# Moving the first norm's squares, small steps and table copies between engines, and deeper fetching in the second convolution

## The chip, the cores and the metric

The kernel runs on one core of a Trainium2 chip. A core has a matrix engine (TensorE, PE in the profile), a vector engine (VectorE, DVE), an activation engine (ScalarE, ACT), a general engine (GpSimd, POOL) and an engine that here only issues transfers (SyncE, SP). They work in parallel, each through its own instructions in order, and wait for each other through semaphores. The metric is the device time of one execution in microseconds. The kernel before took 2557.08 us, the median of three runs (2556.99 to 2560.38).

## The reference

The input x holds 128 images of 128 channels by 16 x 16 points. The part that matters here is the first layer:

- an adaptive group norm of each image: the mean and variance of four channels together, `xn = (x - m) / sqrt(v + eps)`,
- a batch norm over all images, clip to 0..1, rounding to 4 bits, a 3 x 3 convolution with 4-bit weights masked by a pattern,
- a second batch norm, clip, rounding and 3 x 3 convolution with another pattern,
- the sum of that with the normed input as the result of the layer.

The batch norm's mean and variance over all images follow from each image's statistics, so the first convolution can't start before all of x has been read. The layer after it (a two-way state-space mixer with four heads, and a mixture of eight experts) takes the rest of the time.

## The kernel before

**Layout.** Channels lie on the 128 partitions. x stays in the chip's memory as 64 tiles `xr[i]` of two images each (256 KB).

**Setup and first norm (L344 to L511).** SP issues the small inputs, the weights w1 (L364), 64 loads of x (L371), all later weights (`load_weights`, L278 to L307, called at L399), w2 (L401), and then the stores of two tables, `rows_d` and `cols_d` (L489, L490). The tables `rows0` and `cols0` are written by GpSimd (`patterns`, L376 to L397) out of `heads`, `triple`, `ident` and `far`; they go to HBM because the last stage needs copies of them in memory that is not free yet.

For each image VectorE computes statistics (`bn_stats`, L443). For every fourth image below 120 ScalarE does that in two passes: a sum (L441) and, with the negated mean from VectorE (`neg`, L453), a square with a sum (L457). The images are taken in four groups, cut at 48, 96 and 120. ScalarE first takes all sums of a group, then all its squares. For each group VectorE then has some fifteen small steps on tiles of 128 x (images of the group) (L462 to L480), with two matmuls by `grp` (L472, L478) that average over four channels; ScalarE takes the square root (L481), and `normed` (L420 to L434) refines its inverse and derives the scale and shift. `normed` of one group is placed behind the statistics of the next. The last passes (L495 to L511) join all images into the scale `sc1` and shift `bi1` of the first quantising step.

Between these steps VectorE, ScalarE and GpSimd also prepare w1 (`conv_weights`, L138 to L185: tanh, scaling, rounding, masking, and a split into three bf16 parts). The last step writes `how1`, which says which of three forms of the convolution is needed. `by_weights` (L223) reads it on every engine and branches.

**First convolution (conv1, L514).** Per tile: ScalarE or GpSimd applies scale and shift into `q` (L525, L527), VectorE clips and rounds into a padded tile `hpad` (L192), TensorE does five matmuls (L218), ScalarE moves the result to memory (L541), VectorE takes statistics (L542), and SP stores it (L544), except the first eight tiles, which are kept. w2 is prepared along the way. conv1's pools take memory that the setup's pool gives back, the tables among it.

**Second convolution (conv2, L605).** Per tile: SP fetches the stored tile (`fetch`, L618, five tiles ahead, six buffers), ScalarE scales and shifts it in place (L622), VectorE quantises (L192), TensorE convolves (L218), GpSimd or ScalarE prepares the normed input (L663, L665), VectorE adds (L666), TensorE transposes the result (L631), ScalarE copies it into one of three buffers `yt` (L633), and SP stores it (L635). Some steps of the second weights and of the next layer's first tiles are placed between.

**The long stage** (from about 294 us to the end) follows an order written out by hand (the table `T`, L1200). The order in the stages before it is the scheduler's: each engine's list follows the program's order and estimated times, and `tc.issue_after(x)` places steps no earlier than behind x.

Of the kernel before, what the change touches and what calls it, by code (L numbers as in the profile page):

```python
# [34 lines left out]
def kernel(ctx: ExitStack, tc: tile.TileContext, a: dict):  # L35
# [60 lines left out]
    nc.gpsimd.memset(heads, 0.0)  # L96
    nc.gpsimd.memset(triple, 0.0)
    for m in range(2):
        for q in range(3):
            for t in (3 + 4 * q, 15 + 4 * q):  # L100
                nc.gpsimd.affine_select(
                    out=heads, in_=heads, pattern=[[-1, NH]], compare_op=ALU.not_equal,
                    fill=-1.0, base=-(64 + 32 * m + t), channel_multiplier=1,
                )
            nc.gpsimd.affine_select(
                out=triple[:, m : m + 1], in_=triple[:, m : m + 1], pattern=[[0, 1]], compare_op=ALU.not_equal,
                fill=1.0, base=-(64 + 32 * m + q), channel_multiplier=1,
            )
# [114 lines left out]
    def by_weights(how, phase, taps):  # L223

        some = nc.values_load(how[0:1, 0:1], min_val=0, max_val=2)
        with tc.If(some > 0) as cmp:
            with tc.If(some > 1) as cmp2:
                phase(range(9), 3)
            with cmp2.Else():
                phase(range(9), 1)  # L230
        with cmp.Else():
            phase(taps, 1)
# [111 lines left out]
    with tc.tile_pool(name="w1p", bufs=1) as w1p:  # L344

        grp = w1p.tile([P, P], F32, name="grp")
        nc.gpsimd.affine_select(
            out=grp, in_=ones, pattern=[[-4, 32], [0, 4]], compare_op=ALU.is_ge, fill=0.0,
            base=0, channel_multiplier=1,
        )  # L350
        nc.gpsimd.affine_select(
            out=grp, in_=grp, pattern=[[4, 32], [0, 4]], compare_op=ALU.is_ge, fill=0.0,
            base=3, channel_multiplier=-1,
        )
        nc.vector.tensor_scalar(grp, grp, 0.25, None, ALU.mult)
# [4 lines left out]
        with tc.tile_pool(name="setup1", bufs=1) as setup, tc.tile_pool(  # L360
            name="psa", bufs=1, space=PSUM
        ) as psa:
            w1 = w1p.tile([P, 9, P], F32, name="w1", tag="w")
            nc.sync.dma_start(w1, a["L0_conv_w1"])  # L364
            weights = conv_weights(wq1, how1, w1p, psa, w1, pat1, CROSS, "c1")
            for _ in range(3):
                next(weights)


            for i in range(NP):  # L370
                nc.sync.dma_start(xr[i], x_c[:, 2 * i : 2 * i + 2, :])  # L371
            rows0 = setup.tile([P, NH, 2, 2, P], BF16, name="rows0")
            cols0 = setup.tile([P, 2, 2, 2, 2, P], BF16, name="cols0")
            far = setup.tile([HD, 1], BF16, name="far")

            def patterns():  # L376
                nc.gpsimd.memset(far, -1e30)
                for h in range(NH):
                    nc.gpsimd.tensor_copy(
                        rows0[:, h].rearrange("p d t l -> p (d t l)"), heads[:, h : h + 1].to_broadcast([P, 4 * P])  # L380
                    )
                    nc.gpsimd.tensor_copy(
                        rows0[0:HD, h].rearrange("p d t (f l) -> p (d t f) l", l=HD),
                        ident[0:HD, 0:HD].unsqueeze(1).to_broadcast([HD, 2 * 2 * 2, HD]),
                    )
                for m in range(2):
                    for d in range(2):
                        sign = 1 - 2 * d
                        nc.gpsimd.tensor_copy(
                            cols0[:, m, d].rearrange("p j f l -> p (j f l)"), triple[:, m : m + 1].to_broadcast([P, 4 * P])  # L390
                        )
                        for half in range(2):
                            nc.gpsimd.affine_select(
                                out=cols0[0:HD, m, d, :, half, :], in_=far.unsqueeze(2).to_broadcast([HD, 2, P]),
                                pattern=[[0, 2], [sign, P]], compare_op=ALU.is_ge, fill=0.0,
                                base=-sign * HD * half - 1, channel_multiplier=-sign,
                            )  # L397

            load_weights()  # L399
            w2 = w1p.tile([P, 9, P], F32, name="w2", tag="w")  # L400
            nc.sync.dma_start(w2, a["L0_conv_w2"])  # L401

# [11 lines left out]
            cuts = [0, 3 * B // 8, 3 * B // 4, B - max(B // 16, 1), B]  # L414

            def by_scalar(b):

                return b % 4 == 3 and b < cuts[3]

            def normed(c):  # L420

                of = slice(cuts[c], cuts[c + 1])
                var_, gm_, dev_, ga_, qv_, dm_ = (t[:, of] for t in (var, gm, dev, ga, qv, dm))
                nc.vector.reciprocal(ga_, ga_)
                nc.vector.tensor_tensor(dm_, ga_, ga_, ALU.mult)
                nc.vector.tensor_tensor(dm_, dm_, qv_, ALU.mult)
                nc.vector.tensor_scalar(dm_, dm_, -0.5, 1.5, ALU.mult, ALU.add)
                nc.vector.tensor_tensor(ga_, ga_, dm_, ALU.mult)
                nc.vector.scalar_tensor_tensor(shift[:, of], gm_, -1.0, ga_, ALU.mult, ALU.mult)
                nc.gpsimd.tensor_scalar(ares[:, of], ga_, 1.0, SCALE, ALU.add, ALU.mult)  # L430
                nc.gpsimd.tensor_scalar(bres[:, of], shift[:, of], SCALE, None, ALU.mult)
                nc.vector.tensor_tensor(dev_, dev_, ga_, ALU.mult)
                nc.vector.tensor_tensor(var_, var_, ga_, ALU.mult)
                nc.vector.tensor_tensor(var_, var_, ga_, ALU.mult)  # L434

            for c in range(4):
                of = slice(cuts[c], cuts[c + 1])
                for b in range(B)[of]:
                    x_b = xr[b // 2][:, b % 2, :]
                    if by_scalar(b):  # L440
                        nc.scalar.activation(junk, x_b, AF.Copy, accum_out=bst[:, b, 1:2])  # L441
                    else:
                        behind = nc.vector.bn_stats(bst[:, b, :], x_b)  # L443
                if c > 0:

                    with tc.issue_after(behind.ins):
# [3 lines left out]
                if mine:  # L450

                    picked = slice(mine[0], cuts[c + 1], 4)
                    nc.vector.tensor_scalar(neg[:, picked], bst[:, picked, 1], -1.0 / NT, None, ALU.mult)  # L453
                    nc.vector.tensor_scalar(bst[:, picked, 1], neg[:, picked], -1.0, None, ALU.mult)
                    nc.vector.tensor_scalar(bst[:, picked, 4], neg[:, picked], -1.0, None, ALU.mult)
                    for b in mine:
                        nc.scalar.activation(  # L457
                            junk, xr[b // 2][:, b % 2, :], AF.Square, bias=neg[:, b : b + 1],
                            accum_out=bst[:, b, 2:3],
                        )  # L460

                nc.vector.tensor_tensor(mean_, bst[:, of, 1], bst[:, of, 4], ALU.add)  # L462
                nc.vector.tensor_scalar(mean_, mean_, 0.5, None, ALU.mult)
                nc.vector.tensor_tensor(dm_, bst[:, of, 1], bst[:, of, 4], ALU.subtract)
                nc.vector.tensor_tensor(dm_, dm_, dm_, ALU.mult)
# [846 lines left out]
```

## Time and profile before

| | us |
|---|---|
| median of three runs | 2557.08 |
| the profiled execution | 2554.94 |
| its span, first to last instruction | 2553.1 |
| first convolution's first step (ScalarE q) | 85.72 |
| end of the first convolution's statistics (VectorE mv) | 171.4 |
| second convolution's first matmul | 174.74 |
| last transposing of the second convolution | 292.35 |

| engine | busy us | share of the span |
|---|---|---|
| TensorE | 2415.3 | 95% |
| VectorE | 2253.2 | 88% |
| ScalarE | 2173.0 | 85% |
| GpSimd | 1629.3 | 64% |

The shares are averages over stages with different limits. In the first 60 us TensorE is hardly used, the transfers are, and VectorE and ScalarE follow them. The times above are the starts of instructions in the trace, counted from the span's start. A busy time can hold a wait inside an instruction; the idle time before an instruction, and what ended it, are shown apart.

### The profile page before, as it was taken

The page shows a single profiled execution, that of the slowest core. Times are in us where ns is not written, and L with a number is a line of the kernel's source. Part 1 is how long each engine was busy: PE and PEld are TensorE (multiplying, and loading weights), DVE is VectorE, ACT ScalarE, POOL GpSimd, SP SyncE. Part 2 cuts the span into 40 slices and gives each one's busy share as a digit, 9 for nine tenths or more (in the row PEclk, how much of TensorE's full clock was granted, in tenths as well). Part 3 has the DMA queues.
Part 4 walks back from the last instruction along what each step waited for, and adds up shares of the span by engine and source line. Part 5 has one row for each costly group of instructions (what it writes and reads, how often), then busy time and mean ns, then how long its engine had stood idle before and what let it go on. Part 6 is the DMA issues. An engine that isn't in the chain of part 4 may idle for free.

```text
span 2553.1 us, 49290 instructions
## 1 busy us (share of the span) xinstructions
PE 2415.3 (95%) x15940; PEld 1479.9 (58%) x15940; DVE 2253.2 (88%) x6163; ACT 2173.0 (85%) x4455; POOL 1629.3 (64%) x1694
## 2 busy tenths in 40 slices
PE   0688889999999999999999999999999999999997
PEld 0235456666666666666666666666666666666663
DVE  8787699999999999999999999999999999999883
ACT  5678699888889998889898888998988899898881
POOL 3468026676666666666666666666667666666666
PEclk9999899999999999999999999999999999999998
DMA  9358633434444444444444344444433443443343
GB/s 287 124 192 281 227 67 110 125 111 123 130 124 122 122 125 118 120 132 128 120 126 124 114 119 129 128 121 119 129 118 117 132 132 121 123 123 116 107 125 107
DMA packets 302167, 339.58 MB, mean 133 GB/s; under 512 B 56768, under 2 KB 226752, under 8 KB 301888
## 3 DMA queue, kind: packets, MB, share of 16 engines
q1 hardware_dynamic: 301888, 336.21, 43.3%
q8 instruction: 133, 2.18, 0.3%
q14 instruction: 146, 1.20, 0.2%
HBM read 262.72 MB, written 56.62 MB: 125 GB/s over the span
## 4 chain that ended last, share of the span: by engine, by line
PE 88%; DMA 4%; DVE 3%; ACT 2%; issue 1%; SPq 1%; POOL 1%; POOLq 0%; ACTq 0%; DVEq 0%
PE f_ps L1189 17%; PE x_ps L877 13%; PE y_ps L1012 10%; PE z_ps L920 9%; PE o_ps L1072 9%; PE sg L965 5%; PE xt_ps L932 4%; PE y_ps L1018 4%; PE g_ps L951 4%; PE cv L218 4%; DMA xr<-in_x 2%; PE n_ps L1045 1%; PE u_ps L1094 1%; PE f_ps L1184 1%; PE u_ps L750 1%
## 5 line engine op out<-in xcount | busy, mean ns | idle before, releaser
L1177 POOL TENSOR_TENSOR gb<-gb,u2T 128x512 f32<-128x512 f32 x512 | 641.3, 1277 | 122.7 <-PE y_ps L1018 68.8
L895 DVE SCALAR_TENSOR_TENSOR xc<-x_ps,cw,xc 128x510 f32<-128x510 f32 (+2 forms) x768 | 571.7, 744 | 46.5 <-ACT xc L889 36.9
L1028 POOL TENSOR_TENSOR yg<-yg,z 128x512 f32<-128x512 f32 x256 | 325.9, 1279 | 352.1 <-DVE yg L1024 155.1
L1189 PE MATMUL f_ps<-gb,ew 128*128 128x512 f32 x1024 | 510.1, 602 | 6.7 <-POOL gb L1177 6.4
L877 PE MATMUL x_ps<-uT,wx 128*128 128x512 f32 x768 | 402.9, 607 | 7.6 <-ACT e L731 3.3
L731 ACT ACTIVATE e<-sg 128x512 f32<-128x512 f32 x512 | 299.3, 591 | 49.9 <-PE sg L965 44.4
L731 ACT ACTIVATE e<-e,ends 128x128 f32<-128x128 f32 x1024 | 325.0, 392 | 0.0
L1012 PE MATMUL y_ps<-e,xt 128*64 128x256 f32 x2048 | 317.8, 389 | 0.2 <-DVE yg L1024 0.2
L993 DVE TENSOR_TENSOR e<-e,g_ps 128x1024 f32<-128x1024 f32 x256 | 311.6, 1217 | 5.5 <-ACT e L731 2.4
L895 DVE SCALAR_TENSOR_TENSOR bc<-x_ps,cw,bc 128x510 f32<-128x510 f32 (+2 forms) x384 | 286.7, 747 | 20.5 <-ACT bc L889 4.1
L1189 PEld LDWEIGHTS f_ps<-gb,ew 128*128 128x128 f32 x1024 | 180.5, 192 | 174.2 <-issue 136.2
L920 PE MATMUL z_ps<-uT,wz 128*128 128x512 f32 x512 | 271.2, 611 | 1.5 <-ACT xc L889 1.0
L889 ACT ACTIVATE xc<-x_ps,cb,cw 128x512 f32<-128x512 f32 x256 | 199.0, 777 | 64.0 <-PE x_ps L877 57.4
L1072 PE MATMUL o_ps<-wo,yg 128*128 128x128 f32 x2048 | 251.4, 276 | 0.2 <-DVE e L998 0.2
L1072 PEld LDWEIGHTS o_ps<-wo,yg 128*128 128x128 f32 x2048 | 240.5, 193 | 11.1 <-DVE g L1149 8.4
L1024 DVE SCALAR_TENSOR_TENSOR yg<-xc,dcol,y_ps 128x512 f32<-128x512 f32 x256 | 189.8, 742 | 50.1 <-PE y_ps L1018 46.8
L1060 POOL TENSOR_TENSOR rr<-rr,mhalf 128x8 f32<-128x8 f32 x64 | 109.9, 1718 | 161.7 <-DVE g L1151 82.7
L1018 PE MATMUL y_ps<-e,xt 128*64 128x128 f32 x2048 | 199.0, 273 | 0.0
L965 PE MATMUL sg<-rows,cols 128*128 128x256 bf16 x1024 | 192.1, 274 | 5.8 <-ACT e L731 2.8
L1018 PEld LDWEIGHTS y_ps<-e,xt 128*64 128x64 f32 x2048 | 147.0, 137 | 74.1 <-DVE e L998 0.5
L218 PE MATMUL cv<-hpad,wq 128*128 128x512 bf16 x640 | 161.7, 396 | 19.5 <-DVE hpad L192 19.4
L1012 PEld LDWEIGHTS y_ps<-e,xt 128*64 128x64 f32 x2048 | 118.9, 136 | 100.9 <-issue 53.8
(256 smaller groups left out, 4813.9 us busy)
## 6 DMA issues: line engine op xcount, KB each, us to landing
gb<-gd SPq DMA_DIRECT2D x256, 512.0 KB
e<-cum SPq DMA_DIRECT2D x256, 256.0 KB
xr<-in_x SPq DMA_DIRECT2D x64, 256.0 KB
cc<-bc SPq DMA_DIRECT2D x128, 128.0 KB
out<-ob SPq DMA_DIRECT2D x64, 256.0 KB
y<-yt SPq DMA_DIRECT2D x60, 256.0 KB
yt<-y SPq DMA_DIRECT2D x60, 256.0 KB
o<-o SPq DMA_DIRECT2D x56, 256.0 KB
```

The lines of the kernel that those rows point to most:

```text
L731: nc.scalar.activation(out, in_, func, **more)
L877: nc.tensor.matmul(ps, wx[d][:, n * P : (n + 1) * P], uTs[i], start=True, stop=True)
L895: nc.vector.scalar_tensor_tensor(acc[:, :, to], raw[:, :, of], cw[:, d, n, 3 - back : 4 - back], acc[:, :, to], ALU.mult, ALU.add,)
L920: nc.tensor.matmul(ps, wz[:, d, n * P : (n + 1) * P], uTs[i], start=True, stop=True)
L965: nc.tensor.matmul(sg[:, :, of], c_[:, k, d, s, half, :], r_[:, :, d, s, of], start=True, stop=True)
L993: nc.vector.tensor_tensor(e0.rearrange("p h t l -> p h (t l)"), e0.rearrange("p h t l -> p h (t l)"), gps[i, d, k][:, 0:NT].unsqueeze(1).t ...
L1012: nc.tensor.matmul(y_ps[64 * q : 64 * q + 64, k, :], xt[:, 2 * k + s0, 64 * h : 64 * h + 64], e0[:, h].rearrange("p t l -> p (t l)"), star ...
L1018: nc.tensor.matmul(y_ps[64 * q : 64 * q + 64, k, s1 * P : (s1 + 1) * P], xt[:, 2 * k + s1, 64 * h : 64 * h + 64], e1[:, h, :], start=False ...
L1028: large(nc.gpsimd.tensor_tensor(yg, yg, zs[i, d][:, n, :], ALU.mult))
L1072: nc.tensor.matmul(o_ps[:, (2 * j + d) * P : (2 * j + d + 1) * P], ygs[i, d, n][:, t * P : (t + 1) * P], wo[d][:, n, :], start=(n == 0), s ...
L1177: large(nc.gpsimd.tensor_tensor(gb[:, e], gb[:, e], u2Ts[i], ALU.mult))
L1189: nc.tensor.matmul(f_ps, ew[:, e, :], gbs[i, e], start=False, stop=(e == NE - 1))
```

## The change

- Squares: ScalarE takes the square of an image right after the sum of the next one of its images, no longer all squares behind all sums of a group. Each image has its own negation `neg`, on GpSimd.
- Groups: three in place of four, cut at 48 and 112; ScalarE has 28 images in place of 30.
- Small steps: for the first two groups the steps between statistics and scale are GpSimd's, with fused steps taken apart; for the last group they stay on VectorE. ScalarE copies `gm` out of the matmul's result and adds eps itself.
- The reciprocals of the first two groups are placed behind a certain image's statistics, image 78 for the first and image 126 for the second.
- The last six passes (`rs` to `bi1`) are GpSimd's; two products (`b15`, `g15`) are made early.
- Tables: `heads` and `triple` are sums over parts of `ident` on VectorE; `far` is a wider tile; ScalarE copies all of `rows0` and `cols0`, before and after the tanh of w1. Their stores and w2's load are issued right behind x, ahead of `load_weights`.
- `grp` is scaled on GpSimd.
- The kind of weights, `kind(how1)`, is read into registers in the program where `how1` is known.
- conv2: fetches eight tiles ahead, ten buffers.

```diff
-    nc.gpsimd.memset(heads, 0.0)
-    nc.gpsimd.memset(triple, 0.0)
-    for m in range(2):
...
+    strips = ident[:, HD:].rearrange("p (m r) -> p m r", r=32)
+    nc.vector.tensor_reduce(heads, strips[:, :, 3:27].rearrange("p m (u h) -> p h m u", h=NH), AX.XY, ALU.add)
+    nc.vector.tensor_scalar(heads, heads, -1.0, None, ALU.mult)
+    nc.vector.tensor_reduce(triple, strips[:, :, 0:3], AX.X, ALU.add)
...
-        nc.vector.tensor_scalar(grp, grp, 0.25, None, ALU.mult)
+            nc.gpsimd.tensor_scalar(grp, grp, 0.25, None, ALU.mult)
+            far = setup.tile([HD, 2, HD + P], F32, name="far")
...
+            def patterns():
+                nc.scalar.copy(
+                    rows0[:HD].rearrange("p h d j (f l) -> p (h d j f) l", l=HD),
+                    ident[:HD, :HD].unsqueeze(1).to_broadcast([HD, 8 * NH, HD]),
+                )
+                nc.scalar.copy(
+                    rows0[HD:].rearrange("p h d j l -> p h (d j l)"), heads[HD:].unsqueeze(2).to_broadcast([HD, NH, 4 * P])
+                )
+                last = nc.scalar.copy(
+                    cols0[HD:].rearrange("p m d j f l -> p m (d j f l)"), triple[HD:].unsqueeze(2).to_broadcast([HD, 2, 8 * P])
+                )
+                yield last
+                for d in range(2):
+                    for half in range(2):
+                        for m in range(2):
+                            nc.scalar.copy(
+                                cols0[:HD, m, d, :, half, :],
+                                far[:, d, HD - HD * half : HD - HD * half + P].unsqueeze(1).to_broadcast([HD, 2, P]),
+                            )
+                yield
...
             for i in range(NP):
                 nc.sync.dma_start(xr[i], x_c[:, 2 * i : 2 * i + 2, :])
-            load_weights()
+            nc.sync.dma_start(rows_d, rows0)
+            nc.sync.dma_start(cols_d, cols0)
             w2 = w1p.tile([P, 9, P], F32, name="w2", tag="w")
             nc.sync.dma_start(w2, a["L0_conv_w2"])
+            load_weights()
...
-            cuts = [0, 3 * B // 8, 3 * B // 4, B - max(B // 16, 1), B]
+            cuts = [0, 3 * B // 8, 7 * B // 8, B]
...
+                eng = nc.vector if c == 2 else nc.gpsimd
+                eng.tensor_tensor(dm_, ga_, ga_, ALU.mult)
+                eng.tensor_tensor(dm_, dm_, qv_, ALU.mult)
+                eng.tensor_scalar(dm_, dm_, -0.5, 1.5, ALU.mult, ALU.add)
...
+            def squares(most):
+
+                while waiting and most:
+                    b = waiting.pop(0)
+                    nc.scalar.activation(
+                        junk, xr[b // 2][:, b % 2, :], AF.Square, bias=neg[:, b : b + 1], accum_out=bst[:, b, 2:3]
+                    )
+                    most -= 1
...
                     if by_scalar(b):
                         nc.scalar.activation(junk, x_b, AF.Copy, accum_out=bst[:, b, 1:2])
+                        nc.gpsimd.tensor_scalar(neg[:, b : b + 1], bst[:, b, 1:2], -1.0 / NT, None, ALU.mult)
+                        squares(1)
+                        waiting.append(b)
                     else:
-                        behind = nc.vector.bn_stats(bst[:, b, :], x_b)
...
+                        last = nc.vector.bn_stats(bst[:, b, :], x_b)
+                    if b in (cuts[1] + 30, B - 2):
+                        with tc.issue_after(last.ins):
+                            nc.vector.reciprocal(ga[:, cuts[c - 1] : cuts[c]], ga[:, cuts[c - 1] : cuts[c]])
                         normed(c - 1)
...
+                    squares(len(mine))
+                    nc.gpsimd.tensor_scalar(bst[:, picked, 1], neg[:, picked], -1.0, None, ALU.mult)
+                    nc.gpsimd.tensor_scalar(bst[:, picked, 4], neg[:, picked], -1.0, None, ALU.mult)
...
-                nc.vector.tensor_copy(gm_, gm_ps)
-                nc.vector.tensor_tensor(dev_, mean_, gm_, ALU.subtract)
+                nc.scalar.copy(gm_, gm_ps)
+                eng.tensor_tensor(dev_, mean_, gm_ps if c == 2 else gm_, ALU.subtract)
...
-                nc.vector.tensor_scalar(qv_, gv_ps, EPS, None, ALU.add)
-                nc.scalar.activation(ga_, qv_, AF.Sqrt)
+                nc.scalar.activation(ga_, gv_ps, AF.Sqrt, bias=epsc)
+                if c == 2:
+                    nc.vector.tensor_scalar(qv_, gv_ps, EPS, None, ALU.add)
+                    nc.vector.reciprocal(ga_, ga_)
+                else:
+                    nc.scalar.activation(qv_, gv_ps, AF.Identity, bias=epsc)
...
-            rsqrt_eps(rs, bv, EPS)
-
-            nc.vector.tensor_scalar(rs, rs, gam1, NLEV, ALU.mult, ALU.mult)
...
+            nc.gpsimd.tensor_scalar(rs, bv, EPS, None, ALU.add)
+            nc.gpsimd.tensor_tensor(rs, rs, mhalf[:, 0:1], ALU.pow)
+            nc.gpsimd.tensor_tensor(rs, rs, g15, ALU.mult)
+            nc.gpsimd.tensor_scalar(sc1, ga, rs, None, ALU.mult)
+            nc.gpsimd.tensor_scalar(bi1, shift, bm, rs, ALU.subtract, ALU.mult)
+            nc.gpsimd.tensor_scalar(bi1, bi1, b15, None, ALU.add)
...
-                    qs[i] = pc.tile([P, 2, NT], F32, name=f"q2_{i}", tag="q")
+                    qs[i] = pc.tile([P, 2, NT], F32, name=f"q2_{i}", tag="q", bufs=10)
...
-            for i in range(5):
+            for i in range(8):
                 fetch(i)
...
-                fetch(i + 5)
+                fetch(i + 8)
```

## The prediction

> **What bounds the kernel now.** I first read the page: TensorE is busy 95% of the span, and the chain of waits is 88% TensorE. From about 340 us on, a hand-ordered TensorE-bound stage runs to the end. The diff touches nothing there, so what it can move is the time at which that stage starts. Two stages come before it: the load of x with the first norm and first convolution (0 to 172 us), and the second convolution (172 to 292 us). I read the timeline of the first (start, duration, engine, line, tile; in brackets the idle time before and what ended it).
>
> ```profile
> 11.14 7.84 DVE L355 TENSOR_SCALAR grp<-grp 128x128 f32<-128x128 f32 x1
> ...
> 37.95 2.09 DVE L474 TENSOR_TENSOR dev<-mean,gm 128x48 f32<-128x48 f32 x1
> ...
> 61.44 0.24 DVE L466 TENSOR_TENSOR var<-bst 128x48 f32<-128x48 f32 x1 [0.28 <-ACT junk L457]
> ...
> 68.95 0.17 DVE L462 TENSOR_TENSOR mean<-bst 128x8 f32<-128x8 f32 x1
> ...
> 77.33 0.29 DVE L511 TENSOR_SCALAR bi<-bi,b 128x128 f32<-128x128 f32 x1
> ...
> 79.74 0.43 SPq L489 DMA_DIRECT2D rows_d<-rows  x1
> ...
> 85.72 3.23 ACT L525 ACTIVATE q<-xr,bi,sc 128x256 f32<-128x256 f32 x6 [13.64 <-DMA rows_d<-rows]
> ```
>
> The norm is finished at 77.62 (L511), but the first operation of conv1 starts at 85.72: its buffers reuse the setup memory, and the store of rows0 from there is issued at 79.74, behind all weight loads in SP's queue. So 8.1 us are a wait for a late store. Before that VectorE lost 7.8 us at L355 while GpSimd worked, and reached its last image at 68.9. The chain of waits over the load gives what the stage could reach:
>
> ```profile
> 5.02 5.12 DMA xr<-in_x
> 10.15 5.94 DMA xr<-in_x
> ...
> 46.53 6.00 DMA xr<-in_x
> 52.55 6.34 DMA ew<-in_L_ffn_expert_w
> ```
>
> Eight tiles of 256 KB land every 6.0 us, one per 0.75 us: tile k at about 9.4 + 0.75k, tile 63 at about 56.8. VectorE's last image is 12 us behind it.
>
> For the second convolution I took the waits between 178 and 290 us (total, times, longest) and its part of the chain:
>
> ```profile
> DVE xr L666 <- PE cv L218: 17.4, 32, 1.4
> ACT q L622 <- DMA q<-o: 13.7, 16, 1.5
> PEld yt_ps L631 <- ACT yt L633: 9.6, 13, 1.2
> ```
> ```profile
> 194.44 4.92 DMA q<-o
> 199.44 0.67 ACT q L622
> ...
> 214.91 4.55 DMA q<-o
> ...
> 227.89 4.21 DMA q<-o
> ```
>
> ScalarE waits 13.7 us for fetched tiles; TensorE then waits for ScalarE's copies (yt). When nothing waits, the additions L666 come 1.545 us apart. Their first is at 178.88 and the 64th at 291.5: 112.6 us for 63 steps instead of 97.3, so 15.3 us are lost.
>
> **What the Trainium skill says.** GPSIMD Engine Reference, 1 Specifications: GpSimd shares its SBUF interfaces with VectorE, with contention for VectorE instructions in a two-port mode or with two SBUF inputs. The trace agrees: L355 lasts 7.84 us beside GpSimd's table writes, L474 2.09 us beside L184's 2.36 us, where their like take 0.2 to 0.3. ScalarE: Activation LUTs, What ACT_TABLE_LOAD costs: 186 ns + 0.833 ns per element; for 1152 elements that is 1.15 us, and L169 took 1.152. DMA: Bandwidth & Descriptors, Where 436 GB/s comes from: about 358 GB/s per core to HBM; the load of x ran at 349. Advanced Engine Details and Errata, Control Flow Timing: a compare-and-branch costs about 108 ns; but GpSimd's first work of conv2 starts 4.4 us after its last of conv1 ("issue" in the timeline, 173.4 to 177.77), and that number is used.
>
> **The first stage, part by part.** The instruction order of the built kernel says where each step sits.
>
> Tables. GpSimd loses 12 + 6 selections, 12 table copies and 8 selections (about 14 us); ScalarE gets three copies of 2048 elements (each 0.19 + 1.71 = 1.9 us, estimate from the skill's price) and eight of 256 (0.31 apart, near the 0.42 of L441's form). Table load to 2.06, copies to 7.8, tanh as before at 8.68 because w1 lands then, eight small copies to 12.4. Tile 1 landed at 10.15, so ScalarE starts 2.2 us late. VectorE starts at 9.4 instead of 18.9, for the scaling of grp is on GpSimd. It has 100 statistics of 0.335 us (33.5 us) and about 9.5 us of w1's steps in a 47 us load: it stays near the arrivals.
>
> ScalarE in the load. A sum and a square follow each other at 0.54 and 0.63 us, 1.17 per image against 1.50 per arrival, so it catches up by about 20 us. Then it meets steps queued in its order: the cast of w1 waits for VectorE's w, which comes after tile 24 (27.4) plus 1.35: 29.3, done at 30.4. A sum and two squares: 32.2. Its new copy of gm waits for five GpSimd steps (0.35 each, below) and a matmul: 33.9. Two sums, the 1.28 us table load, sqrt and the second copy: 36.8. Square and cast: 38.6; then the third cast waits for GpSimd's 2.36 us subtraction and ends at 42.2. Tile 33, next in line, landed at 34.2. Left are 12 sums and 14 squares: 6.5 + 8.8 = 15.3, to 57.5. GpSimd's eleven steps for the first group stand before some of its negations, which ScalarE's squares need: 1 us more, 58.5. So ScalarE, not the load, ends the second group.
>
> GpSimd steps. No row has 128x64 on it. Nearest rows:
>
> ```profile
> L596 POOL TENSOR_TENSOR nmra<-mva,rstda 128x4 f32<-128x4 f32 x64 | 15.3, 240 | 4.9
> L431 POOL TENSOR_SCALAR bres<-shift 128x48 f32<-128x48 f32 x2 | 0.7, 344 | 0.2
> L184 POOL TENSOR_TENSOR w<-t_c,wq 128x1152 f32<-128x1152 f32 x2 | 4.9, 2448 | 18.7 <-ACT wq L183 18.7
> ```
>
> Between 0.24 and about 0.52 (the line through 1.28 for 512 elements and 2.36 for 1152), I take 0.35 with gaps, and 0.6 as the bad end for contention. After the sum of tile 55 (57.2): negation and five steps to the mean, 59.3; matmul and ScalarE's copy, 60.2; five steps, 62.0; matmul and sqrt, 62.9. VectorE's reciprocal (0.55) stands before its last statistics, so that statistic, waiting behind the sqrt though its tile landed at 56.8, ends at 63.9. From there the last group took 68.95 to 75.61 before, 6.7 us; I add 0.7 for ScalarE's copy and for VectorE's two-input steps beside GpSimd's eleven for group two (63.5 to 67.4): 71.3. The last six passes on GpSimd: 0.2, 0.58 (the power, L133), 0.26, three of 128x128 at about 0.4, gaps 0.5: 2.7, where VectorE with the power took 2.0. So 74.0, and conv1 at 74.1: a gain of 11.6.
>
> Stores of the tables. They now stand right behind x in SP's queue, are issued when tile 56 has landed (52.6) and took 5.9 us before: down by about 60. w2 waits for w1's last cast (42.2), no delay at 53; the small weights go to 79 as now, and the first store of conv1 is wanted only at tile 8, about 85. Cost nothing; if SP were later, five o1 buffers cover 6 us.
>
> GpSimd's jump into conv1 now comes after its last pass: first work 4.3 us after the start instead of 1.3. Tile 3 is its first; the first ten matmuls took 4.28 us (87.33 on) and tile 3 was due 7 us in: cost nothing, 2 us if not covered. The early read of the kind of weights changes no engine's order: nothing. Conv1 itself is unchanged.
>
> **The second convolution.** Ten fetch buffers for six. A buffer comes free when its tile is quantised, then 4 to 5 us of fetch: six tiles at 1.545 are 9.3 us, and ScalarE runs ahead of the quantising VectorE by one or two tiles; ten give 15.5. At the start SP stood 12.7 us before it could fetch on (DMA at 0 to 94 GB/s around 181 to 189 us); four more tiles use that gap. Between zero and all 13.7 us can go. Of the 15.3 lost I count as the fetches' the stalls at 199 (1.9), 219 (2.5), 232 (about 2), 245 to 252 (about 1.7 of 4.9, the rest is the early norm's GpSimd and ScalarE steps) and 269 (0.9): 9.0. Full pace needs 512 KB per 1.545 us, 339 GB/s, near the 349 seen, so I don't take more.
>
> **Sum.** 11.6 + 9.0 = 20.6 us, carried through to the end since TensorE bounds the rest. The profiled execution took 2554.94 (span 2553.1 and 1.8 around it): 2534.3. The median of the runs is 2.1 above it: 2536.5.
>
> **Rivals.** (1) The fetches aren't cured, because stores and fetches share a saturated DMA: 0.7 to 0.89 busy speaks for it, streaks of seven tiles at 1.545 against. Only 11.6 remain: 2545.5. (2) GpSimd becomes the bound of the norm: seventeen of its small steps lie on the path to 74; at 0.7 us each instead of 0.35, 6 us more: 2542.5. The 2.09 us of L474 speaks for contention; the nmra row against. (3) Slower: a y store needs one of three yt buffers. Its turn is its landing time L plus 1 us for copy and issue; three buffers give (L+1)/3 per tile. The chain shows L = 3.63 at 247.5 (1.54). If fetches in flight stretch L, conv2 loses more than conv1's start gained from 1.84 + 11.6/64 = 2.02 us per tile, L = 5.1; at L = 6, 2.33 x 64 = 149 against 117.6: 2577. Against it: one fetch per tile is issued as before, only earlier. (4) ScalarE keeps up and the load bounds: 56.8 + 0.5 + 6.7 + 2.2 = 66.2, 8 us better, with all 13.7 of conv2: 2524. (5) The change doesn't take effect: conv1's first step still waits, for a later load counted on the same queue, about 85: only conv2's 9 remain, 2548.
>
> **How the numbers follow.** The forecast has 0.62 (14 to 27 us: 2530 to 2543), rival 1 0.12, rival 2 0.08, rival 4 0.08, rival 3 0.05, rival 5 and the mixtures with under 5 us of gain 0.05. This kernel's measurement can't tell 0.2% (5.1 us) from nothing. All but the last two are faster: 0.90, same 0.05, slower 0.05. The range 2527 to 2547 leaves out half of rival 4, rival 3, rival 5 and a part of the forecast's edges.
>
> **What would show it.** ScalarE's first q of conv1 near 74, its wait ended by GpSimd's bi and not by rows_d; VectorE's first statistics near 9.5; ScalarE's last square of the second group near 58; small GpSimd steps near 0.35; conv2's steps near 1.65 us and ACT q's wait for q under 4 us. I am wrong if y stores take over 5 us, if VectorE's steps after 62 us stretch beside GpSimd, or if the long stage starts earlier but ends no earlier.

## The result and the profile after

The changed kernel takes 2543.47 us, the median of four runs (2541.67 to 2545.61), against 2557.30 for the kernel before beside it (four runs, 2556.99 to 2560.38). The ratio is 0.9944, with a 95% interval of 0.9926 to 0.9961: 13.8 us faster. I had forecast 20.6. The time lies in the range; both parts of the sum are smaller than I had them, and one of them for a reason that I had not seen. It also lies just outside 2530 to 2543, where I had put the forecast itself: the range holds it because it was left wide for the rivals.

| | before | after | earlier by |
|---|---|---|---|
| profiled execution, its span | 2554.94, 2553.1 | 2543.71, 2542.0 | 11.1 (span) |
| conv1's first step (ScalarE q) | 85.72 | 75.79 | 9.9 |
| conv1's first matmul | 87.33 | 77.40 | 9.9 |
| VectorE starts to join conv1's statistics (mv) | 169.47 | 159.28 | 10.2 |
| first addition of conv2 | 178.88 | 167.94 | 10.9 |
| 64th addition of conv2 | 291.46 | 279.31 | 12.2 |
| end of conv2's last copy yt | 293.66 | 281.51 | 12.2 |

The first stage gave 9.9 us in these two executions, conv2 1.2 from its first to its 64th addition (112.6 to 111.4). The 171.4 that I gave for mv ahead of the prediction is its end, not its start. The profiled execution of before was 2.4 us below the median of its four runs, that of after at its own. The long stage, which no version here touches, took 2258.6 to 2262.1 us in the profiles of this study (from the end of conv2's last copy yt to the end of the span), so two single executions can't be compared to better than about 3.5 us.

The timeline of the changed kernel's first stage (start, duration, engine, line, tile; in brackets the idle time before and what ended it):

```profile
9.60 1.10 DVE L469 BATCH_NORM_STATS2 bst<-xr 128x6 f32<-128x256 f32 x3 [4.18 <-DMA xr<-in_x]
...
32.32 1.50 POOL L483 TENSOR_TENSOR mean<-bst 128x48 f32<-128x48 f32 x1
...
35.16 0.20 ACT L495 COPY gm<-gm_ps 128x48 f32<-128x48 f32 x1 [2.42 <-PE gm_ps L494]
...
58.27 0.42 ACT L464 ACTIVATE junk<-xr 128x256 f32<-128x256 f32 x1
...
59.56 0.51 ACT L453 ACTIVATE junk<-xr,neg 128x256 f32<-128x256 f32 x1
...
61.51 0.36 POOL L488 TENSOR_TENSOR var<-bst 128x64 f32<-128x64 f32 x1
...
64.61 0.55 DVE L472 RECIPROCAL ga<-ga 128x64 f32<-128x64 f32 x1 [7.17 <-ACT ga L502]
...
65.08 0.37 DVE L469 BATCH_NORM_STATS2 bst<-xr 128x6 f32<-128x256 f32 x1
...
74.23 0.81 POOL L532 TENSOR_SCALAR bi<-shift,bm,rs 128x128 f32<-128x128 f32 x1
75.14 0.61 POOL L533 TENSOR_SCALAR bi<-bi,b 128x128 f32<-128x128 f32 x1
75.79 3.06 ACT L547 ACTIVATE q<-xr,bi,sc 128x256 f32<-128x256 f32 x6 [7.09 <-POOL bi L533]
```

VectorE starts 9.3 us sooner (18.90 before). The last line is what the change did to the stage: the first q follows the norm's last pass within 0.1 us, where it had stood 8.1 us more for the store of `rows_d`. That store is now issued at 51.88. The lines of L483 and L495 and GpSimd's last two, L532 and L533, are where it came short of the forecast.

The waits in conv2 of the changed kernel, between 168 and 280 us (total, times, longest):

```profile
DVE xr L688 <- PE cv L209: 15.6, 31, 1.3
ACT yt L655 <- PE yt_ps L653: 13.6, 14, 2.5
ACT q L644 <- DMA q<-o: 8.0, 9, 2.3
PEld yt_ps L653 <- ACT yt L655: 5.8, 9, 2.1
```

and the fetches and stores in its chain of waits:

```profile
200.55 4.17 DMA q<-o
...
215.50 5.39 DMA q<-o
...
237.60 3.77 DMA y<-yt
```

ScalarE still waits 8.0 us for fetched tiles, and fetches still stand in the chain at places (205, 220) where TensorE waits for copies yt, although ten tiles can now be under way.

### The profile page after: what moved, and what is told of

Read it like the earlier page. It is cut to its first block, busy times and chain, and to the rows that moved or that the text cites. A ratio compares the mean times of both kernels' runs of the same rounds, so it can differ in the third digit from the quotient of the medians.

```text
span 2542.0 us, 49262 instructions
## 1 busy us (share of the span) xinstructions
PE 2412.9 (95%) x15936; PEld 1481.2 (58%) x15936; DVE 2239.5 (88%) x6094; ACT 2178.8 (86%) x4462; POOL 1639.8 (65%) x1733
## 4 chain that ended last, share of the span: by engine, by line
PE 90%; DVE 3%; ACT 2%; issue 1%; DMA 1%; POOL 1%; SPq 0%; ACTq 0%; POOLq 0%; DVEq 0%
PE f_ps L1211 17%; PE x_ps L899 13%; PE y_ps L1034 10%; PE z_ps L942 9%; PE o_ps L1094 9%; PE sg L987 5%; PE xt_ps L954 4%; PE y_ps L1040 4%; PE g_ps L973 4%; PE cv L209 4%; PE n_ps L1067 1%; PE u_ps L1116 1%; PE f_ps L1206 1%; PE u_ps L772 1%; PE rt_ps L1123 1%; PE yt_ps L653 1%
## 5 line engine op out<-in xcount | busy, mean ns | idle before, releaser
L917 DVE SCALAR_TENSOR_TENSOR bc<-x_ps,cw,bc 128x510 f32<-128x510 f32 (+2 forms) x384 | 286.5, 746 | 20.6 <-ACT bc L911 4.5
L1094 PEld LDWEIGHTS o_ps<-wo,yg 128*128 128x128 f32 x2048 | 240.5, 193 | 11.1 <-DVE g L1171 8.4
L1040 PEld LDWEIGHTS y_ps<-e,xt 128*64 128x64 f32 x2048 | 147.0, 137 | 74.1 <-DVE e L1020 0.5
L209 PE MATMUL cv<-hpad,wq 128*128 128x512 bf16 x640 | 162.3, 398 | 12.8 <-DVE hpad L183 12.7
```

Source lines behind the costliest of these rows:

```text
L917: nc.vector.scalar_tensor_tensor(acc[:, :, to], raw[:, :, of], cw[:, d, n, 3 - back : 4 - back], acc[:, :, to], ALU.mult, ALU.add,)
L1040: nc.tensor.matmul(y_ps[64 * q : 64 * q + 64, k, s1 * P : (s1 + 1) * P], xt[:, 2 * k + s1, 64 * h : 64 * h + 64], e1[:, h, :], start=False ...
L1094: nc.tensor.matmul(o_ps[:, (2 * j + d) * P : (2 * j + d + 1) * P], ygs[i, d, n][:, t * P : (t + 1) * P], wo[d][:, n, :], start=(n == 0), s ...
```

## The question, and what the order shows

Each tile k of conv2 has a fetch, an activation q on ScalarE and, when its convolution is added, a copy yt, also on ScalarE. The instruction order of the built kernels tells how they stand in ScalarE's list. In the steady part of the form that ran, the last q ahead of the copy yt of tile j is that of tile j + 8 (sometimes j + 9) before, and of tile j + 12 (sometimes j + 13) after. Four more buffers, and the scheduler put q four tiles further ahead. Measured from tile to tile, the time from a fetch's issue to the start of its q is 5.0 us on average before and 6.4 after, and from q to the quantising step on VectorE 5.2 before and 10.6 after. Most of the new slack lies behind q, where nobody waits for a transfer. The timeline of the changed kernel shows what it costs (lines of ScalarE, then of TensorE):

```profile
220.49 0.81 ACT L644 ACTIVATE q<-q,bi,sc 128x512 f32<-128x512 f32 x1 [2.27 <-DMA q<-o]
221.21 0.57 ACT L655 ACTIVATE yt<-yt_ps 128x512 f32<-128x512 f32 x1
...
221.84 0.66 PE L653 MATMUL yt_ps<-ident,xr 128*128 128x128 f32 x4 [1.57 <-ACT yt L655]
```

The q here is tile 40's, quantised only at 235.19. The copy behind it is tile 28's, added at 215.75, and TensorE, which needs its bank of the matmul memory, stands 1.57 us for it. ScalarE stands in order at a fetch that nothing needs for another 14 us. This is the largest stall of conv2: the addition of tile 32 follows the one before it after 7.23 us, where the steady step is 1.545.

So theory A: the order on ScalarE ate the deeper fetch. Its rivals: theory B, the deeper fetch brought its 9 us and another part of the change lost 7; theory C, my rival of the saturated DMA.

## Experiments on the second convolution

**Fetch depth undone.** The changed kernel with six buffers.

```diff
-                    qs[i] = pc.tile([P, 2, NT], F32, name=f"q2_{i}", tag="q", bufs=10)
+                    qs[i] = pc.tile([P, 2, NT], F32, name=f"q2_{i}", tag="q")
...
-            for i in range(8):
+            for i in range(5):
...
-                fetch(i + 8)
+                fetch(i + 5)
```

> The changed kernel with six fetch buffers and five tiles fetched ahead in the second convolution, as in the kernel before. Theory A (the order on ScalarE ate the deeper fetch: its rescaling of tile k stands 12 tiles ahead of the copy yt with ten buffers, 8 with six, so a fetch has about 4.5 us either way): almost nothing is lost, first to 64th addition about 112.5 us instead of 111.4, time 2544 to 2546. Theory B (ten buffers did bring the 9 us that I forecast, and another part of the change cost 7 us in conv2): the loss is the whole 9, about 2552.

Measured: 2547.80 us (2544.22 to 2549.09, six runs), ratio to before 0.9965 (0.9953 to 0.9978). That is 4.3 us above the changed kernel. It lies between the theories, nearer A; theory B's 2552 is excluded. The depth was worth some 4 us, and since the two ratios have intervals of this width, anything from nothing to 10 us is possible. In its profiled execution, the highest of the six, ScalarE waited 18.6 us for q and the additions spread over 117.9 us. That is 5.3 us more than in the profile of the kernel before, with the same six buffers and again a lead of 8 tiles. What made that one execution longer is open, so the weighing of A against B here rests on the medians; the experiments on the order decide it.

**ScalarE's order mended.** The changed kernel with ten buffers; q of tile k may not stand ahead of the copy yt of tile k-7.

```diff
+            yts_done = {}
...
                 q = qs.pop(i)
-                nc.scalar.activation(q, q, AF.Identity, bias=bi2, scale=sc2)
+                if i - 7 in yts_done:
+                    with tc.issue_after(yts_done[i - 7].ins):
+                        nc.scalar.activation(q, q, AF.Identity, bias=bi2, scale=sc2)
+                else:
+                    nc.scalar.activation(q, q, AF.Identity, bias=bi2, scale=sc2)
...
-                nc.scalar.activation(yt.rearrange("p t c -> p (t c)"), yt_ps, AF.Copy, scale=1.0 / SCALE)
+                yts_done[i] = nc.scalar.activation(yt.rearrange("p t c -> p (t c)"), yt_ps, AF.Copy, scale=1.0 / SCALE)
```

> The changed kernel, with ScalarE's rescaling of tile k of conv2 put behind its copy yt of tile k-7 in its own order; ten buffers stay. Theory A: ScalarE no longer stands at a fetch that it does not need yet (its waits for q fall from 8.0 us to under 1), the copies yt come in time, and first to 64th addition falls from 111.4 to between 100 and 104 us: 2532 to 2536. Theory C (the DMA is full: fetches and stores of 512 KB per step can't go faster): the waits only move, 110 us or more, 2541 to 2545.

Measured: 2538.38 us (2536.96 to 2540.12, four runs), ratio 0.9932 (0.9916 to 0.9949). The additions take 106.3 us instead of 111.4, and ScalarE's waits for q are gone altogether. The direction is A's, the size about half of what I expected; theory C, which wanted 110 us or more, falls. Its waits in conv2, and the store in its chain of waits, show what came in place of the fetches:

```profile
ACT yt L660 <- PE yt_ps L658: 9.8, 14, 1.8
ACT yt L660 <- DMA y<-yt: 8.1, 8, 1.8
```
```profile
184.50 5.15 DMA y<-yt
```

ScalarE now waits for one of three buffers yt to be stored. That is the mechanism of my third rival, and the 5.15 us of this one store lie just above the 5.1 that I had named as the point from which it decides. It does not set the pace of every tile: the rival's sum asks for over 2.02 us per tile, and the additions come 1.69 us apart on average.

**Order mended, depth undone.** Both edits above.

> Both edits: ScalarE's rescaling of tile k behind its copy of tile k-7, and six buffers with five ahead. Theory A in its strong form (order alone is what counts; with six buffers a fetch is issued some nine steps before the addition of its tile, lands after 4 to 5 us and is wanted about 6 us after its issue): 102 to 106 us from first to 64th addition, 2534 to 2539. If depth counts once the order is right: 107 to 111, 2539 to 2544.

Measured: 2538.25 us (2537.16 to 2539.31), ratio 0.9928 (0.9911 to 0.9945), 106.7 us of additions, no wait for q. With the order mended six buffers do as well as ten; at six buffers, mending the order brings 9.5 us (2547.80 to 2538.25). Fetch to q is 7.1 us now, with the same six buffers that gave 5.0.

**The same in the kernel before**, with nothing else of the change.

> The kernel before, nothing of the change in it, with ScalarE's rescaling of tile k of conv2 put behind its copy of tile k-7; its six buffers stay. If the order is the whole cause of the fetch waits: ScalarE's wait for q goes from 13.7 us to under 1, first to 64th addition 105 to 107 us instead of 112.6, and 9 us less time as between the two runs with six buffers on the changed kernel, 2547 to 2549. If the deeper fetch or something else of the change has a part in it: 2552 or more.

Measured: 2548.75 us (2547.22 to 2550.63, six runs) against 2557.43 beside it, ratio 0.9965 (0.9953 to 0.9978): 8.7 us, and 105.5 us of additions instead of 112.6. No wait for q is left in its conv2, only

```profile
ACT yt L638 <- DMA y<-yt: 7.4, 7, 1.9
```

So nearly all of the 9 us that I had put down to the fetch waits were there to be had, by an edit of the order alone.

**Six buffers for the copies**, on the version with the order mended and six fetch buffers.

```diff
-                yt = yts[i] if i in yts else pc.tile([P, 4, P], F32, name=f"yt_{i}", tag="yt", bufs=3)
+                yt = yts[i] if i in yts else pc.tile([P, 4, P], F32, name=f"yt_{i}", tag="yt", bufs=6)
...
-            u = pc.tile([P, 4, P], F32, name=f"u{i}", tag="yt", bufs=3)
+            u = pc.tile([P, 4, P], F32, name=f"u{i}", tag="yt", bufs=6)
```

> ScalarE's order mended (rescaling of tile k behind the copy of tile k-7), six fetch buffers, and six buffers instead of three for the copies yt that are stored. With the order mended ScalarE waits 4 to 8 us for y stores, which land after 5.2 us. If three buffers are the limit (my rival of the y stores): these waits go, first to 64th addition 102 to 104 us, 2533 to 2536. If the DMA is full: 106 us as with three buffers, 2538, and a wait for q or y comes elsewhere.

Measured: 2537.49 us (2536.51 to 2539.26), ratio 0.9926 (0.9910 to 0.9943); the additions take 105.8 us. The waits for y stores are gone, but only 1 us of the 2.7 to 4.7 that I expected came: other steps stand in their place. The busy times of its stretches (the stretch and its length, busy us and instructions of TensorE, its weight loads, VectorE, ScalarE and GpSimd, then TensorE's clock, DMA share, GB/s):

```profile
189.00:232.00 43.00, 43.00 (x248) 25.89 (x247) 35.06 (x63) 38.39 (x67) 43.00 (x71) 1.00 0.96 325
232.00:238.00 6.00, 3.40 (x20) 1.95 (x19) 6.00 (x21) 3.52 (x7) 5.18 (x10) 0.93 0.50 151
```

For 43 us TensorE (the first busy time) shows no idle time while the DMA moves 325 GB/s at a busy share of 0.96: TensorE doesn't wait for it there, close to full though it is. Then, from 231.26 to 235.5, VectorE (the third) makes twenty small constants for the next layer ahead of its addition, and TensorE stands: the addition of tile 40 comes 4.0 us late. With shorter stalls at the additions of tiles 24 and 32 (1.2 us each), where TensorE and VectorE prepare the expert weights, these make up most of the 8.5 us still lost against 97.3.

**Four banks for the transposes**, on the changed kernel.

```diff
-        ) as psc, tc.tile_pool(name="psw", bufs=2, space=PSUM) as psw:
+        ) as psc, tc.tile_pool(name="psw", bufs=4, space=PSUM) as psw:
```

> The changed kernel with four PSUM banks instead of two for the transposes of conv2; ScalarE's order and the fetches stay. The copies yt come up to 7.8 us after their addition, and a bank covers one step of 1.54 us. If late copies stop TensorE by its banks: first to 64th addition from 111.4 to 106 to 109 us, 2538 to 2541, and ScalarE still waits for q. If the waits lie elsewhere: no change.

Measured: 2540.68 us (2538.33 to 2544.00), ratio 0.9933 (0.9917 to 0.9950). The median is 2.8 us lower, but the runs of the two overlap, and in the profiled execution, the highest of the four, the additions still take 109.7 us and ScalarE waits 12.0 us for q. This is inconclusive; banks cover late copies at best in part.

**All three together**: order mended, six buffers for q and for yt, four banks (the edits above).

> As the run before it (order mended, six buffers for q and for yt), and four PSUM banks for the transposes. What is then left of TensorE's waits for copies yt, about 5 us, goes too: first to 64th addition 98 to 101 us, near the 97.3 of 63 steps at 1.545, and 2530 to 2533. If the DMA is full: 104 or more, 2536 or more.

With the order mended and six buffers, four banks change nothing: 2537.79 us (2534.76 to 2540.69), ratio 0.9922 (0.9906 to 0.9939), 106.1 us of additions. I had expected 98 to 101: I had put the rest down to late copies. The largest stall is the same as in the version before: the addition of tile 40 comes 4.7 us late, behind the same twenty steps of VectorE.

## Experiments on the first stage

**The table stores last again**, behind w2 and all small weights. The load of w2 keeps its place ahead of the small weights; in the kernel before it stood behind them, right before the stores.

```diff
-            nc.sync.dma_start(rows_d, rows0)
-            nc.sync.dma_start(cols_d, cols0)
             w2 = w1p.tile([P, 9, P], F32, name="w2", tag="w")
             nc.sync.dma_start(w2, a["L0_conv_w2"])
             load_weights()
+            nc.sync.dma_start(rows_d, rows0)
+            nc.sync.dma_start(cols_d, cols0)
```

> The changed kernel with the two stores of the tables behind the second convolution's weights and all small weights in SP's queue, as before. If the late store was the wait that held conv1 (my step of 8.1 us): the store is issued near 79, ScalarE's first q comes near 85 ended by rows_d, and all of the first stage's 9.9 us is lost: 2552 to 2555. If something else held the first q (a load on the same queue, as in my rival of no effect), it stays near 76 and the time near 2543.5.

Measured: 2552.96 us (2548.58 to 2555.56, 20 runs), ratio 0.9982 (0.9975 to 0.9989), which is 9.5 us above the changed kernel. In the profiles the first q comes 8.0 us later. The timeline of SP's queue and ScalarE in this version:

```profile
80.63 0.47 SPq L403 DMA_DIRECT2D rows_d<-rows  x1
...
83.78 3.31 ACT L547 ACTIVATE q<-xr,bi,sc 128x256 f32<-128x256 f32 x6 [15.30 <-DMA rows_d<-rows]
```

Without the early place of these two stores in SP's queue nearly all of the first stage's gain is gone. The norm itself being ready sooner is worth nothing while they stand late. The first q does come 1.9 us before that of the kernel before (85.72), but because the store is done sooner: the first q follows its issue by 3.2 us here and by 6.0 in the kernel before (6.1 in the profile of that kernel with the order mended). There the 576 KB of w2 were requested 0.7 us ahead of the store, here long before; that this makes the difference is likely, but not tried. The opposite edit, the stores moved in the kernel before and nothing else, was not run. There the norm ended at 77.62, so by my estimate it could bring at most 8.1 of the 9.9 us; the rest needs the norm to be ready sooner.

**Five of the last six passes on VectorE again** (the power stays on GpSimd).

```diff
-            nc.gpsimd.tensor_scalar(rs, bv, EPS, None, ALU.add)
+            nc.vector.tensor_scalar(rs, bv, EPS, None, ALU.add)
...
-            nc.gpsimd.tensor_tensor(rs, rs, g15, ALU.mult)
-            nc.gpsimd.tensor_scalar(sc1, ga, rs, None, ALU.mult)
-            nc.gpsimd.tensor_scalar(bi1, shift, bm, rs, ALU.subtract, ALU.mult)
-            nc.gpsimd.tensor_scalar(bi1, bi1, b15, None, ALU.add)
+            nc.vector.tensor_tensor(rs, rs, g15, ALU.mult)
+            nc.vector.tensor_scalar(sc1, ga, rs, None, ALU.mult)
+            nc.vector.tensor_scalar(bi1, shift, bm, rs, ALU.subtract, ALU.mult)
+            nc.vector.tensor_scalar(bi1, bi1, b15, None, ALU.add)
```

> The changed kernel with five of the first norm's last six passes on VectorE again, the power alone on GpSimd. GpSimd took 3.4 us for the six (0.61, 0.81 and 0.61 for the three of 128x128), VectorE had 2.0 before. If the move itself was a loss: ScalarE's first q of conv1 at 74.3 to 74.6 instead of 75.8, about 1.3 us less time, 2542. If it paid by what it left VectorE free for: 76 or later.

Measured: 2544.71 us (2542.33 to 2545.89), ratio 0.9951 (0.9935 to 0.9968). No gain: 1.2 us above the changed kernel, within the runs' spread. The first q did come 1.6 us sooner, but the first matmul 0.85 us later. The timeline of this version, then the changed kernel's:

```profile
74.23 3.06 ACT L547 ACTIVATE q<-xr,bi,sc 128x256 f32<-128x256 f32 x6 [5.56 <-DVE bi L533]
...
77.51 0.16 DVE L202 TENSOR_SCALAR less<-less_ps 128x1 f32<-128x1 f32 x1 [3.32 <-issue]
...
78.25 1.01 PE L209 MATMUL cv<-hpad,wq 128*128 128x512 bf16 x2 [5.57 <-DVE hpad L183]
```
```profile
76.03 0.16 DVE L202 TENSOR_SCALAR less<-less_ps 128x1 f32<-128x1 f32 x1 [3.75 <-issue]
...
77.40 1.86 PE L209 MATMUL cv<-hpad,wq 128*128 128x512 bf16 x4 [4.64 <-DVE hpad L183]
```

VectorE too needs 3.3 to 3.8 us from its last pass to its first step in conv1, a stretch in which it waits for nothing that the trace shows. In the changed kernel it is done at 72.28 and spends that time while GpSimd makes the last passes; with the passes its own, the stretch begins at 74.2 and TensorE's first tile waits for it.

**The first group's later steps put behind more sums** on ScalarE, on the version with six buffers for q and yt.

```diff
-                        nc.scalar.activation(junk, x_b, AF.Copy, accum_out=bst[:, b, 1:2])
+                        summed = nc.scalar.activation(junk, x_b, AF.Copy, accum_out=bst[:, b, 1:2])
...
+                    if b in (cuts[1] + 8, cuts[1] + 9, cuts[1] + 16):
+                        with tc.issue_after(summed.ins):
+                            next(first_group)
```

Here `first_group` is a generator (the rest of the edit only sets it up) that holds the first group's steps from the matmul by `grp` to the square root, in three parts.

> The best version so far (order mended, six buffers for q and for yt) with ScalarE's copy of gm, square root and second copy of the first norm's first group put four sums later in its order, so that it no longer stands 2.4 us for GpSimd's step of 1.50 us. If ScalarE's work ends the second group, as my forecast had it: its last square ends about 2 us sooner (58 instead of 60.2), the first q of conv1 comes at 73.5 to 74.2 instead of 75.7, and about 1.8 us less time, 2535.7. If VectorE or GpSimd ends it: 75 to 76, and no change.

Measured: 2539.68 us (2536.74 to 2540.71), ratio 0.9928 (0.9911 to 0.9944), no gain over 2537.49. In the timeline:

```profile
34.95 0.20 ACT L455 COPY gm<-gm_ps 128x48 f32<-128x48 f32 x1 [1.34 <-PE gm_ps L454]
...
39.57 1.15 ACT L176 CAST wq<-w 128x1152 bf16<-128x1152 f32 x1 [1.61 <-POOL w L175]
```

The edit freed little: the wait for gm fell from 2.42 to 1.34 us, and that for GpSimd's subtraction rose from 0.84 to 1.61. Against the version that it was made on, ScalarE's last sum of the second group starts at 57.80 instead of 58.11, and the first q at 75.34 instead of 75.64, 0.3 us sooner each. The size that I expected failed, and 75.34 lies where I had expected it if ScalarE did not end the group; 0.3 us alone decide nothing. The traces do: in the changed kernel and the seven versions that keep both the early stores and the last six passes on GpSimd, the first q follows the start of that last sum after 17.5 us each time, whether the sum starts at 57.80 or at 58.27.

## Why the prediction was right or wrong

**The late store: right.** The store left at 51.88 (I had 52.6), cost nothing, and the first q waits for `bi` alone. Undoing it costs 9.5 us.

**The start of the load: right.** VectorE's first statistics at 9.60 (9.4), ScalarE's first sum at 12.54 (12.4).

**ScalarE ends the second group: right, 1.6 us too early.** What counts is its last sum, from which I had let GpSimd's steps start: it ended at 58.78, where I had 57.2. The last square ended at 60.17 for 58.5, but nothing waited for it: the step of GpSimd that needs it (`var`, L488, at 61.51) stands behind others and starts without a wait. The cast of w1 ended its wait at 29.79 for 29.3. The copy of gm came at 35.16 for 33.9, because one of GpSimd's five steps, L483, took 1.50 us and not 0.35. It started while VectorE ran a two-input step of 1.34 us; the Trainium skill (GPSIMD Engine Reference, 1 Specifications) has the two engines share their interfaces to SBUF, which fits these two numbers, though VectorE's step kept its length (1.36 in the kernel before, with GpSimd idle) and no run here took the one step away. All other small steps on 128 x 48 and 128 x 64 were 0.23 to 0.38, so the price itself held, and rival 2, with 0.7 for every step, did not come. The other term is the pair of a sum and a square: 1.235 us when they alternate, for the 1.17 that I had added up from runs of equal ones. The 1 us for a negation behind GpSimd's eleven steps came as 0.99.

**The tail: 0.6 us better, the last six passes 0.7 worse.** From the end of VectorE's last statistics (65.45 for 63.9) to `bv` it took 6.8 us, where I had 7.4. The six passes took 3.4 us from 72.36, where I had 2.7: the three of 128 x 128 on GpSimd took 0.61, 0.81 and 0.61, and my 0.4 was a line through wider tiles. Together 75.79 for 74.1, a gain of 9.9 where I had 11.6. One term I took as given: VectorE stood 7.17 us for the square root of the second group ahead of its last statistic (L472), though that tile had landed by 57.5, and the last group's steps came only after it. What an earlier place of that statistic and of these steps would bring was not tried.

**GpSimd's jump: hidden, as said.** I had not counted that VectorE makes the same jump on the path. The move of the passes to GpSimd is what hides it, so the part of the change that I had booked as a loss of 0.7 us is about even.

**conv1 unchanged: right.** From its first matmul to mv 81.9 us, 82.1 before.

**Conv2: wrong, about 4 us for 9.0.** The step that failed is "ScalarE runs ahead of the quantising VectorE by one or two tiles". Its q stood 5.2 us ahead of the quantising step before and 10.6 after, which at the 1.79 and 1.77 us per tile of these executions is about three tiles and six, for its place in the order follows the number of buffers. I had counted the buffers between the fetch and the quantising step, and took the whole of it to be the fetch's. (The 12.7 us for which I let SP stand at the start is the length of a row of three issues; the next fetch left 10.2 us after the one at 176.0.) The indicators said so: a step of 1.77 us (111.4 by 63) for 1.65, and 8.0 us of waits for q for under 4. The 9.0 us itself was well sized: mending the order brought 9.5 us on the changed kernel with six buffers and 8.7 on the kernel before.

**The rivals.** Rival 1 had nearly the time (2545.5) and the wrong cause: with the same transfers the waits for q vanish when the order is mended, and with six buffers yt as well the DMA carries 325 GB/s over 43 us in which TensorE is never idle. Rival 3 did not decide, but its mechanism was real, and stood behind the fetch waits. Rivals 4 and 5 did not come: ScalarE did not keep up, and the change does what it says.

**The sum.** By medians 9.5 us hang on the first stage (before against the version with the depth undone; the stores put back cost as much) and 4.3 on the deeper fetch, for 11.6 and 9.0. The best version found, with the order mended and six buffers for q and yt, takes 2537.49 us, 6.0 below the changed kernel; the other versions with the order mended on the changed kernel can't be told from it.

## What to carry to other kernels

A deeper buffer is meant for the gap between a transfer and its first user; where a scheduler or an in-order list decides how early that user stands, look at the order before adding buffers, for the user may move ahead with them and hold up what is queued behind it. Ask of every wait for a transfer whether the waiting step is needed yet, and put it behind the work that is. And before taking steps off an engine or giving them back, see what the engine does next: a stretch like the 3 to 4 us around the branch here can be on the path or hidden, depending on who has that last step.

## What the runs showed of the hardware that I had not expected

- VectorE has 3.3 to 4.0 us without a visible cause between its last step before the branch into conv1 and its first behind it in the profiles of the changed kernel and its versions, as GpSimd has 4.4 into conv2 in the kernel before (3.0 to 3.6 in the other profiles). The reading of the kind of weights and the branch lie there. Their records in the changed kernel (duration in ns, then the start in us; a q behind the engine's name stands for its sequencer):

```profile
L216 DVEq TENSOR_LOAD <-how x1: 543/543/543, 72.1 to 72.1; - x1
L219 DVEq COMPARE_BRANCH  x1: 72/72/72, 72.8 to 72.8; - x1
L219 PEldq COMPARE_BRANCH  x1: 3988/3988/3988, 68.4 to 68.4; - x1
```

VectorE's read and branch are over by 72.9 and its next step starts at 76.03, although the matmul that it needs was done at 72.8: most of the time lies behind the recorded branch. On TensorE the branch itself is recorded with 3.99 us. What fills this time no trace here shows.
- With TensorE idle for some microseconds in conv2, its next matmuls run slower for a while: five took 2.34 us at 225.16 in the changed kernel, 1.27 in the steady part, and the granted clock was 0.89 over 219 to 234 us and 1.00 in the stretches around it. That stall cost about 1 us more than its own length.
- The long stage, with the same instructions each time, took 2258.6 to 2262.1 us from one profiled execution to the next, more than some of the effects looked for here.
